# Four layers over one adjacency matrix: the order of the first loads on the sync queue

## The chip, the cores and the metric

One core of a Trainium2 chip runs the whole program. The metric is the device time of one launch in microseconds; beside it stands one execution taken by the hardware profiler. The engines are PE (matrix products), DVE (vector), ACT (scalar), POOL and SP; SP only issues transfers here, ACT issued two in the kernel before, and POOL issues the indirect ones. All transfers run on 16 DMA engines.

## What is computed

A graph of 2708 nodes, 512 features each, with a weighted, sparse adjacency matrix `adj` (2708 x 2708, float32). Four layers, each adds its result to x after a layer norm and a relu:

```
h = relu(layernorm(x));  x = x + L0(h, adj)     # (adj + head) @ h / row sum,  head = mask / |mask|
h = relu(layernorm(x));  x = x + L1(h, adj)     # attention of 8 heads, with Wv and Wo
h = relu(layernorm(x));  x = x + L2(h, adj)     # two adjacency layers and a tanh
h = relu(layernorm(x));  x = x + L3(h, adj)     # (adj != 0) @ (h W + b) / degree
```

The diagonal of `adj` is always there. In L1 the kernel multiplies Wv by Wo once (`wvo`) and reads, for each node, one row of h @ wvo.

## The kernel before, in words

**Tiles.** Nodes are cut into 22 tiles of 128 rows (the last has 20). Layer 0, the part that the change touches, runs a loop over node tiles m from 0 to 21 and needs, for each: the slab `ar` (128 rows of adj, 128 x 2708, 1.39 MB, line 563), from which ACT makes signs (L583), counts and row sums (L611) and DVE the two largest of a row and their places (`attended`, L623 and L624, one pass each); blocks `at` of the transposed adj (128 x 4 x 128, 256 KB, L680), from which DVE makes the left operand `inc` (L698, L706); and the normed rows `h` of x (tiles h0 to h21).

**Three dense tiles, then lists.** For m = 0, 1, 2 (LEAD is 3) the product takes all 22 row tiles: six to seven blocks `at` each, two PE instructions for a row tile (L866). From m = 3 on it takes a few dense row tiles, and the rest is gathered: ranks of nonzero columns (counts by PE at L325, scan at L405, write and read back by SP at L409 and L445, search by DVE at L461) give indices, by which POOL gathers pieces of adj (L635) and rows of h from `h0d` (L654) into the buffers that held h6 to h21. `h0d` is the stored copy of the normed rows (L492, issued by POOL).

**The opening.** Before the loop over m stands a sequence written out by hand. It loads Wv and Wo on the ACT queue (L499, L503), slab 0, four row tiles of x, slab 3, six more tiles of x, slab 4, and the last twelve tiles of x, all on SP (L485, L563). Then it norms rows: statistics on DVE (L194, L196), a square root on ACT (L198), reciprocal and shift on DVE (L199, L201), and the norm with relu on ACT (L204). `value_weights` transposes Wv on PE (L514), copies it to SBUF on DVE (L517), multiplies it by Wo on PE (L176) and copies the product `wvo` out on ACT (L521). `stats_to` does a slab's signs and sums; slabs come in the order 0, 3, 4, 5, 1, 2, 6, 7 and so on.

**What sets the order.** The tile framework takes the operations as the program states them and plans each engine's list ahead, with its own estimate of times; on the chip every engine, and SP's queue too, works its list strictly in order and stands still at the first instruction whose inputs are not there. Slabs have three buffers, blocks `at` three, `inc` three. A transfer also waits until an earlier one that used the same completion counter has landed: transfers of SP and ACT take eight counters in turn, so the ninth waits for the first.

Of the kernel before, what the change touches and what calls it, by code (L numbers as in the profile page):

```python
# [9 lines left out]
FP = mybir.dt.float32  # L10
# [12 lines left out]
P = 128  # L23
# [21 lines left out]
def kernel(  # L45
# [27 lines left out]
    nc = tc.nc  # L73

    N, D = x.shape
    H, _, DK = wk_d.shape
    NT = (N + P - 1) // P
# [12 lines left out]
    def rows(t):  # L90
        return min(P, N - t * P)

    def dense_of(m):

        return WHOLE[m]

    def alone(m):

        return DENSE <= m < NFULL
# [70 lines left out]
    def span(t):  # L170
        return slice(t * P, t * P + rows(t))

    def project(acc, hT, n, w):

        for c in range(NCD):
            nc.tensor.matmul(  # L176
                acc[:n], hT[:, c, :n], w[:, c, :], start=(c == 0), stop=(c == NCD - 1)
            )
# [65 lines left out]
    with tc.tile_pool(name="l0_slab", bufs=2) as slabs, tc.tile_pool(  # L244
        name="l0_h", bufs=1
    ) as hp, tc.tile_pool(name="l0_w", bufs=2) as wp, tc.tile_pool(
        name="l0_acc", bufs=2, space=PSUM
    ) as ps_acc, tc.tile_pool(name="l0_small", bufs=1, space=PSUM) as ps_small, tc.tile_pool(
        name="l0_list", bufs=3, space=PSUM
    ) as ps_list, tc.tile_pool(name="l0_tr", bufs=1, space=PSUM) as ps_tr, tc.tile_pool(  # L250
        name="l0_y", bufs=1, space=PSUM
# [228 lines left out]
        h0 = {}  # L480

        def load_h0(ts):
            for t in ts:
                h0[t] = hp.tile([P, D], FP, name=f"h{t}")
                nc.sync.dma_start(out=h0[t][: rows(t)], in_=x[span(t)])  # L485

        def norm_h0(ts):
# [8 lines left out]
        wo = wset.tile([P, NCD, D], FP, name="wa1")  # L496

        def load_values():
            nc.scalar.dma_start(  # L499
                out=wv.rearrange("p h c k -> p h (c k)"),  # L500
                in_=wv_d.rearrange("h (p c) k -> p h (c k)", c=NCD),
            )
            nc.scalar.dma_start(out=wo, in_=wo_d.rearrange("(c p) k -> p c k", p=P))  # L503

        def value_weights():

            wvo = hp.tile([P, NCD, D], FP, name="wvo")
            wvt = wset.tile([P, NCD, D], FP, name="wa2")
            for r in range(NCD):
                pt = ps_tr.tile([P, NCD, P], FP, name="pt")  # L510
                for c in range(NCD):
                    for k in range(0, P, DK):
                        head = wv[:, (r * P + k) // DK, c, :]
                        nc.tensor.matmul(  # L514
                            pt[k : k + DK, c, :], head, ident, start=True, stop=True
                        )
                nc.vector.tensor_copy(wvt[:, r, :].rearrange("k (p c) -> k c p", c=NCD), pt)  # L517
            for r in range(NCD):
                acc = ps_y.tile([P, D], FP, name="yacc")
                project(acc, wvt[:, :, r * P : (r + 1) * P], P, wo)  # L520
                nc.scalar.copy(wvo[:, r, :], acc)  # L521
            return wvo
# [30 lines left out]
        FIRST = list(range(LEAD, LEAD + GROUP))  # L553
# [4 lines left out]
        def load_slab(m):  # L558
            n = rows(m)
            if m in slab:  # L560
                return
            slab[m] = slabs.tile([P, N], FP, name="ar", bufs=3)
            nc.sync.dma_start(out=slab[m][:n], in_=adj[m * P : m * P + n])  # L563
# [124 lines left out]
        def incidence(m):  # L688

            n = rows(m)  # L690
            rn = row[m][0]
            rb = ps_small.tile([P, P], FP, name="rb")
            nc.tensor.matmul(
                rb[:, :n], rn[:n].to_broadcast([n, P]), ident[:n, :n], start=True, stop=True
            )

            def add_head(inc, a, k, num):
                nc.vector.scalar_tensor_tensor(  # L698
                    inc,
                    a,  # L700
                    0.0,
                    rb[:k, :n].unsqueeze(1).to_broadcast([k, num, n]),
                    op0=ALU.is_gt,
                    op1=ALU.mult,
                )
                nc.vector.tensor_tensor(inc, inc, a, ALU.add)  # L706

            pairs = []
            if m >= LEAD:
                ts = tiles_d[: dense_of(m)]  # L710
                pieces = [ts[i : i + PIECE0] for i in range(0, len(ts), PIECE0)]
            else:
                pieces = in_order if m + 1 < LEAD else dense_last
            for ts in pieces:
                at, k = blocks.pop(m) if m in blocks else load_block(m, ts)
                d = (slice(0, k), slice(0, len(ts)), slice(0, n))
                inc = slabs.tile([P, PIECE0, P], FP, name="inc", bufs=3)
                add_head(inc[d], at[d], k, len(ts))
                pairs += [(inc[:k, i, :n], h0[t][:k]) for i, t in enumerate(ts)]
            if alone(m):  # L720
                c = diag_c[:, m : m + 1]
                by = wp.tile([P, 3], FP, name="by")
                nc.scalar.activation(by[:, 2:3], c, AF.Sign)
                nc.scalar.activation(by[:, 2:3], by[:, 2:3], AF.Identity, scale=rn, bias=c)
                nc.scalar.activation(by[:, :2], kept[:, :, m], AF.Copy, scale=by[:, 2:3])
                own = wp.tile([P, D], FP, name="own", bufs=1)
                nc.scalar.activation(own, xs[m], AF.Relu, scale=by[:, 0:1], bias=by[:, 1:2])
                pairs.append((ident, own))
            if m >= LEAD:
                ac, gs = gathers.pop(m)  # L730
                pending.append(lambda: nc.sync.dma_start(out=listed[m], in_=ac))
                inc = slabs.tile([P, NCL, P], FP, name="incl")[:, : CHUNKS[m], :n]
                add_head(inc, ac, P, CHUNKS[m])

                nc.vector.tensor_tensor(
                    ac[:1, 0, :1], ac[:1, 0, :1], inc[:1, 0, :1], ALU.min
                )
                pairs += [(inc[:, c, :], g) for c, g in enumerate(gs)]
            return pairs
# [22 lines left out]
        def stats_to(m):  # L762


            while normed[0] <= order_n.index(m):
                t = order_n[normed[0]]
                do_next()
                load_slab(t)
                if normed[0] + 1 < NT:
                    load_slab(order_n[normed[0] + 1])  # L770
                row_norm(t)
                row_sum(t)
                if t == 0 or t % GROUP == GROUP - 1 or t >= NT - 2:
                    last_block = count(masks)
                    if t not in ZERO:
                        if dense_of(t):
                            rank_blocks(list(masks), last_block)
                        else:
                            flush_counts()
                            todo.append(partial(rank_rows, list(masks)))  # L780
                        todo.extend(partial(search, k) for k in masks)
                        do_next(0)
                    masks.clear()
                if t in LATE:
                    slab.pop(t)
                else:
                    attended(t)
                normed[0] += 1
# [40 lines left out]
        def flush():  # L829
# [2 lines left out]
                issue()  # L832
            pending.clear()

        load_values()
        load_slab(0)
        load_h0(range(4))
        load_slab(FIRST[0])
        load_h0(range(4, 10))
        load_slab(FIRST[1])  # L840
        load_h0(range(10, NT))
        stats_to(0)
        norm_h0(range(4))
        incs, hns, xs, hTs = {0: incidence(0)}, {}, {}, {}
        stats_to(FIRST[0])
        wvo = value_weights()
        norm_h0(range(4, 10))
        stats_to(FIRST[1])
        norm_h0(range(10, 16))
# [562 lines left out]
    FIRST = 2  # L1412
# [86 lines left out]
    for i, m in enumerate(order_3):  # L1499
# [6 lines left out]
        if i + AHEAD < len(order_3):  # L1506
            k = order_3[i + AHEAD]
# [19 lines left out]
    with tc.If(general > 0):  # L1527

        with tc.tile_pool(name="l0_g", bufs=2) as gp, tc.tile_pool(
            name="l0_gh", bufs=1  # L1530
        ) as hp, tc.tile_pool(name="l0_gps", bufs=2, space=PSUM) as ps:
            hs = []
            for t in range(NT):
# [3 lines left out]
                h = hp.tile([P, D], FP, name=f"h{t}")  # L1537
                norm(gp, xt, n, h, AF.Relu)
                hs.append(h)
            for m in range(NT):  # L1540
# [23 lines left out]
                for t in range(NT):  # L1564
                    k = rows(t)
# [18 lines left out]
        with tc.tile_pool(name="l1_qkv", bufs=1) as qkvp:  # L1584
# [3 lines left out]
            wo = load_w(qkvp, wo_d, "wo")  # L1588
            qk_scale = float(DK) ** -0.5

            with tc.tile_pool(name="l1_pw", bufs=1) as pwp, tc.tile_pool(
                name="l1_ph", bufs=2
            ) as php, tc.tile_pool(name="l1_px", bufs=3) as pxp, tc.tile_pool(
                name="l1_pps", bufs=2, space=PSUM
# [4 lines left out]
                for w, src in ((wk, wk_d), (wq, wq_d), (wv, wv_d)):  # L1599
                    for h in range(H):  # L1600
                        nc.sync.dma_start(
                            out=w[:, :, h * DK : (h + 1) * DK],
                            in_=src[h].rearrange("(c p) k -> p c k", p=P),
# [34 lines left out]
            with tc.tile_pool(name="l1_bias", bufs=2) as bp, tc.tile_pool(  # L1638
                name="l1_p", bufs=2
            ) as pp, tc.tile_pool(name="l1_pT", bufs=3) as ptp, tc.tile_pool(  # L1640
                name="l1_x", bufs=1
            ) as xp, tc.tile_pool(name="l1_st", bufs=4) as stp, tc.tile_pool(
                name="l1_s", bufs=2, space=PSUM
            ) as ps_s, tc.tile_pool(name="l1_t", bufs=2, space=PSUM) as ps_t, tc.tile_pool(
                name="l1_o", bufs=1, space=PSUM
            ) as ps_o, tc.tile_pool(name="l1_y", bufs=1, space=PSUM) as ps_y:
                SW = 2 * BLK
                for m in range(NT):
# [11 lines left out]
                    for h in range(H):  # L1660
                        oc, r0 = divmod(h * DK, P)
                        p = pp.tile([P, N], FP, name="p")
# [21 lines left out]
                        for t0 in range(0, NT, 4):  # L1684
# [3 lines left out]
                            for t in ts:  # L1688
                                k = rows(t)
# [9 lines left out]
                            for t in ts:  # L1699
                                k = rows(t)  # L1700
# [29 lines left out]
        with ExitStack() as gen:  # L1730
# [3 lines left out]
            hp = gen.enter_context(tc.tile_pool(name="hp", bufs=2))  # L1734
# [218 lines left out]
```

## Time and profile before

| | us |
|---|---|
| runs of the kernel before (5) | 1421.26 to 1431.37, median 1429.03 |
| profiled execution, its own time | 1432.48 |
| its span | 1430.7 |
| layer 0, up to the last row combine | 0 to 500 |
| busy in the span: PE, DVE, ACT, POOL | 1216.1, 925.4, 693.7, 675.2 |
| busy from 0 to 80: PE, DVE, ACT, POOL | 53.57, 43.30, 58.27, 17.43 |
| tile 0 combined, tile 1, tile 2, tile 3 (L879) | 79.25, 104.86, 145.89, 170.7 |

A line of the timeline holds start, duration, engine, line, operation, output<-inputs, form and count; in brackets stands the engine's idle time before it and what ended it. A line of the waits holds the waiting instruction, what it waited for, total us, times, and the longest. "SPq" is SP's queue of transfers. From 0 to 80 us the trace counts 28.63 MB moved at a DMA share of 0.98. PE's granted clock is 1.0 in most stretches and 0.5 in short ones.

### The profile page before, as it was taken

What the parts mean: (1) busy time and instruction counts of PE and PEld (TensorE: products, weight loads), DVE (VectorE), ACT (ScalarE), POOL (GpSimd) and SP (SyncE); (2) the same over time, 40 slices, a digit from 0 to 9 for tenths busy, and PEclk for the clock granted to TensorE, in tenths of its full rate; (3) what the DMA queues carried; (4) which work ended last, traced back from release to release, by engine and by line L of the source; (5) the groups of instructions that cost most, each with busy time, mean ns of one, the idle gap of its engine ahead of it and who ended that gap; (6) DMA issues with size and microseconds to landing.
All of it is one profiled execution on the core that took longest, in us unless ns stands there. A gap on an engine that the chain in (4) does not pass through costs nothing. (4 is left out here: it accounts for less than half of the span.)

```text
span 1430.7 us, 15148 instructions
## 1 busy us (share of the span) xinstructions
PE 1216.1 (85%) x4223; PEld 722.0 (50%) x4223; DVE 925.4 (65%) x1859; ACT 693.7 (48%) x1098; POOL 675.2 (47%) x703
## 2 busy tenths in 40 slices
PE   4877976859686938999989999899999999958797
PEld 2333433324333415765655665466656666636575
DVE  4676984859699957963444445456577776737576
ACT  5865353647536446642333223244555554625453
POOL 2255465555558351106554553245435444167663
PEclk9988998889898968999999999999999999979999
DMA  9986887778869659728887878766656656488885
GB/s 340 371 278 229 301 280 236 258 238 309 273 202 319 234 193 318 243 92 267 263 281 233 279 250 258 255 205 201 215 166 217 201 191 208 141 312 253 262 243 168
DMA packets 179341, 349.92 MB, mean 245 GB/s; under 512 B 22794, under 2 KB 85524, under 8 KB 175516
## 3 DMA queue, kind: packets, MB, share of 16 engines
q1 hardware_dynamic: 131648, 201.72, 41.5%
q0 software_dynamic: 46032, 145.05, 31.7%
q10 hardware_dynamic: 1568, 2.10, 0.4%
q8 instruction: 35, 0.57, 0.2%
q14 instruction: 58, 0.48, 0.1%
HBM read 285.97 MB, written 62.82 MB: 244 GB/s over the span
## 5 line engine op out<-in xcount | busy, mean ns | idle before, releaser
L1047 POOL DMA_INDIRECT gg<-g2d,idx_g x130 | 146.2, 1125 | 190.5 <-PE aggs L1110 141.8
L1110 PE MATMUL aggs<-gg,ac 128*128 128x512 f32 (+1 forms) x520 | 231.5, 594 | 2.6 <-DMA gg<-g1d,idx_g 2.5
L1047 POOL DMA_INDIRECT gg<-g1d,idx_g x130 | 131.8, 1014 | 157.1 <-PE aggs L1110 83.4
L635 POOL DMA_INDIRECT ac<-in_adj_t_dram,idx_a x130 | 135.1, 1039 | 94.7 <-issue 45.2
L866 PE MATMUL acc<-h,inc 128*128 128x512 f32 (+1 forms) x276 | 138.8, 647 | 35.1 <-DVE inc L706 28.7
L654 POOL DMA_INDIRECT h<-h0d,idx_g x111 | 113.2, 1020 | 90.0 <-issue 34.4
L1110 PEld LDWEIGHTS aggs<-gg,ac 128*128 128x128 f32 (+1 forms) x520 | 97.4, 189 | 113.1 <-issue 100.0
L866 PE MATMUL acc<-h,incl 128*128 128x512 f32 (+1 forms) x222 | 109.4, 634 | 5.8 <-issue 5.8
L866 PEld LDWEIGHTS acc<-h,inc 128*128 128x128 f32 (+1 forms) x276 | 53.3, 206 | 95.9 <-issue 55.6
L176 PE MATMUL yacc<-wvo,hT 128*128 128x512 f32 (+1 forms) x176 | 87.0, 634 | 7.0 <-ACT hT L211 6.3
L1047 POOL DMA_INDIRECT gg<-hidr,idx_g x62 | 65.6, 1057 | 37.6 <-issue 18.0
L1075 DVE SCALAR_TENSOR_TENSOR ac<-ac,diag_c,bias 128x512 f32<-128x512 f32 x30 | 22.5, 751 | 89.3 <-DMA ac<-g1d 50.4
L1106 PE MATMUL agg<-ghi,a_hi 128*128 128x512 f32 x180 | 76.4, 424 | 0.0
L1106 PE MATMUL agg<-glo,a_lo 128*128 128x512 f32 x180 | 72.6, 403 | 4.4 <-ACT glo L225 4.4
L1106 PE MATMUL aggs<-gs,a_s 128*128 128x512 f32 x180 | 72.5, 403 | 1.7 <-DVE gs L222 1.3
L866 PEld LDWEIGHTS acc<-h,incl 128*128 128x128 f32 (+1 forms) x222 | 43.0, 200 | 57.5 <-issue 53.6
L990 DVE SCALAR_TENSOR_TENSOR v_lo<-pt,v_hi 128x512 fp32r<-128x512 f32 (+1 forms) x88 | 56.9, 657 | 15.3 <-ACT v_hi L989 12.1
L623 DVE MAX8 tops<-ar 128x8 f32<-128x2708 f32 (+1 forms) x22 | 65.3, 2970 | 0.0
L624 DVE FIND_INDEX8 at_top<-tops,ar 128x8 uint32<-128x2708 f32 (+1 forms) x22 | 65.3, 2968 | 0.0
L1139 DVE SCALAR_TENSOR_TENSOR u<-aggs,u 128x512 f32<-128x512 f32 x42 | 28.9, 688 | 53.2 <-PE aggs L1110 39.7
L989 ACT ACTIVATE v_hi<-pt 128x512 fp32r<-128x512 f32 (+1 forms) x88 | 48.2, 575 | 29.2 <-PE pt L983 21.6
L176 PEld LDWEIGHTS yacc<-wvo,hT 128*128 128x128 f32 (+1 forms) x176 | 34.6, 201 | 51.5 <-issue 43.7
(355 smaller groups left out, 2788.3 us busy)
## 6 DMA issues: line engine op xcount, KB each, us to landing
ar<-in_adj_dram SPq DMA_DIRECT2D x27, 1354.0 KB
raw<-in_adj_t_dram SPq DMA_DIRECT2D x92, 192.0 KB
slot<-x SPq DMA_DIRECT2D x41, 256.0 KB
at<-in_adj_t_dram SPq DMA_DIRECT2D x26, 256.0 KB
h<-in_x_dram SPq DMA_DIRECT2D x21, 256.0 KB
h0d<-h POOLq DMA_DIRECT2D x21, 256.0 KB
xt<-in_x_dram SPq DMA_DIRECT2D x21, 256.0 KB
x<-xt SPq DMA_DIRECT2D x21, 256.0 KB
```

The source lines that it names most:

```text
L176: nc.tensor.matmul(acc[:n], hT[:, c, :n], w[:, c, :], start=(c == 0), stop=(c == NCD - 1))
L623: nc.vector.max(tops[:n, m, :], ar[:n])
L624: nc.vector.max_index(at_top[:n, m, :], tops[:n, m, :], ar[:n])
L635: nc.gpsimd.indirect_dma_start(out=ac[:, c, :n], out_offset=None, in_=adj_units, element_offset=dense_of(m) * P * N + m * P, in_offset=bas ...
L654: nc.gpsimd.indirect_dma_start(out=g, out_offset=None, in_=h0d[:, :], in_offset=bass.IndirectOffsetOnAxis(ap=index_g(m)[:, c : c + 1], axi ...
L866: product = nc.tensor.matmul(acc[:n], a, g, start=(i == 0), stop=(i == len(pairs) - 1))
L989: nc.scalar.activation(hi[d], pt[d], AF.Relu, scale=UP)
L990: nc.vector.scalar_tensor_tensor(lo[d], pt[d], 0.0, hi[d].bitcast(FP), op0=ALU.max, op1=ALU.subtract)
L1047: nc.gpsimd.indirect_dma_start(out=gs[c], out_offset=None, in_=gd[:, :], in_offset=bass.IndirectOffsetOnAxis(ap=index_g(m)[:, c : c + 1], ...
L1106: turn(nc.tensor.matmul(acc[:n], a[:k, i, :n], b[:k], start=st, stop=sp))
L1110: nc.tensor.matmul(mixed[:n], a, g, start=(c == 0 and not dense_of(m)), stop=(c == len(chunks) - 1),)
L1139: done = nc.vector.scalar_tensor_tensor(u[:n], mixed[:n], EPS12, u[:n], op0=ALU.mult, op1=ALU.add)
```

## The change

Wv becomes the first transfer of SP's queue instead of ACT's. Wo goes to SP as well, behind the first four tiles of x. The request for slab 4 and for the last twelve tiles of x is stated behind slab 0's statistics, the norm of the first four tiles and the operand of tile 0, so that the first blocks `at` of tile 0 are requested ahead of those twelve. `value_weights` is stated ahead of slab 3's statistics instead of behind. The buffers h0 to h21 are made in front of all loads, since the operand of tile 0 names them.

```diff
         def load_h0(ts):
             for t in ts:
-                h0[t] = hp.tile([P, D], FP, name=f"h{t}")
                 nc.sync.dma_start(out=h0[t][: rows(t)], in_=x[span(t)])
...
         def load_values():
-            nc.scalar.dma_start(
+            nc.sync.dma_start(
                 out=wv.rearrange("p h c k -> p h (c k)"),
                 in_=wv_d.rearrange("h (p c) k -> p h (c k)", c=NCD),
             )
-            nc.scalar.dma_start(out=wo, in_=wo_d.rearrange("(c p) k -> p c k", p=P))
+
+        def load_output():
+            nc.sync.dma_start(out=wo, in_=wo_d.rearrange("(c p) k -> p c k", p=P))
...
+        for t in range(NT):
+            h0[t] = hp.tile([P, D], FP, name=f"h{t}")
         load_values()
         load_slab(0)
         load_h0(range(4))
+        load_output()
         load_slab(FIRST[0])
         load_h0(range(4, 10))
-        load_slab(FIRST[1])
-        load_h0(range(10, NT))
         stats_to(0)
         norm_h0(range(4))
         incs, hns, xs, hTs = {0: incidence(0)}, {}, {}, {}
+        load_slab(FIRST[1])
+        load_h0(range(10, NT))
+        wvo = value_weights()
         stats_to(FIRST[0])
-        wvo = value_weights()
         norm_h0(range(4, 10))
```

FIRST is the list 3, 4, 5. The order that the framework plans from this, on SP: Wv, slab 0, x 0 to 3, Wo, slab 3, x 4 to 9, three blocks of tile 0, slab 4, three more blocks (the third of one row tile), x 10 to 16, the seventh block, x 17 to 21, slab 5, slab 1. Before, it was: slab 0, x 0 to 3, slab 3, x 4 to 9, slab 4, x 10 to 21, three blocks, slab 5, three more blocks, slab 1, the seventh block. On the other engines the planned order differs as well, in all of layer 0 up to about tile 18.

## The prediction, as it was put on record

> **What bounds the kernel now.** I started from the page's busy rows and then cut the span into its stages. Layer 0 fills 0 to 500 us, and only there does the built order of instructions differ between the two kernels (on DVE the last difference stands near row 656 of some 4630, at node tile 18 of 0 to 21; behind it both run the same list). So the question is what limits layer 0, above all its opening. Busy time of stretches of the kernel before; the columns are busy us (and instructions) of PE, weight load, DVE, ACT and POOL, then granted clock, DMA share and GB/s:
>
> ```profile
> 12.00:24.00 12.00, 7.00 (x48) 4.50 (x48) 3.75 (x12) 2.91 (x6) 0.00 (x0) 1.00 0.91 330
> 24.00:80.00 56.00, 46.57 (x140) 18.22 (x139) 36.07 (x125) 49.17 (x78) 11.92 (x22) 0.91 1.02 373
> 99.00:125.00 26.00, 14.37 (x32) 5.62 (x34) 14.27 (x30) 7.61 (x14) 17.20 (x19) 0.74 0.58 182
> 125.00:146.00 21.00, 18.55 (x57) 8.28 (x54) 13.52 (x20) 14.37 (x17) 8.97 (x10) 0.84 0.88 302
> ```
>
> The reader is to see three things. From 24 to 80 us ACT works 49.17 of 56 us and the DMA share is 1.02: both are close to full. From 12 to 24 us ACT works 2.91 of 12 us, so 9.1 us are open there. From 99 to 125 us nothing is full: PE 14.37 of 26, ACT 7.61, DMA 0.58.
>
> Why ACT stands still before 24 us is told by the waits of the opening (PE, then SP's queue) and by the timelines of DVE and ACT:
>
> ```profile
> PE pt L514 <- DMA wa<-in_L_gnn_Wvs_dram: 15.9, 1, 15.9
> ...
> SPq L485 <- DMA wa<-in_L_gnn_Wvs_dram: 11.8, 1, 11.8
> ```
> ```profile
> 17.87 1.05 DVE L517 COPY wa<-pt 128x512 f32<-128x512 f32 x1 [5.69 <-PE pt L514]
> 18.77 0.15 DVE L585 TENSOR_SCALAR sum_sgn<-sum_sgn 128x1 f32<-128x1 f32 x1
> ```
> ```profile
> 13.48 0.19 ACT L611 ACTIVATION_READ_ACCUMULATOR ar<-ar 128x1 f32 x1
> 19.04 0.29 ACT L588 ACTIVATE rn<-sum_sgn,tiny 128x1 f32<-128x1 f32 x1 [5.37 <-DVE kept L199]
> 23.05 0.57 ACT L341 CAST counts<-list 128x485 bf16<-128x485 f32 x1 [3.72 <-PE list L325]
> ```
>
> Read backwards: ACT waits 5.37 us for a small DVE result; DVE cannot reach it because the copy of the transposed Wv (L517) stands in front and waits 5.69 us for PE; PE waits for Wv until 15.86. ACT's second wait, 3.72 us, is for the counts of slab 0, which stand on PE behind the same Wv products. SP is held too: its fifth row of x waits 11.8 us until Wv has landed.
>
> **The change part by part.** Time is counted against the profiled execution: span 1430.7 us, time 1432.48 us. It lies 3.45 us over the median of the runs, 1429.03; the sum is made on the former and taken off the latter.
>
> *Wv to the head of SP's queue.* In the DMA view of 0 to 80 us, the ACT queue (q10), which carries Wv and Wo alone, takes 7.5% of 16 engines: 0.075 x 80 = 6.0 us for both, 3.0 us for Wv. Placed first, Wv pushes slab 0 back by at most that: the first sign (L583) starts at 7.06 + 3.0 = 10.06 us instead of 7.06. This is a cost. The DVE statistics that stand behind the Wv copy now follow within that time, and the waits of 5.37 and 3.72 us go. From 10.06, ACT works through what it did from 7.06 to 13.67 (6.61 us, to 16.7), then rn 0.29, counts 0.83, three norms of x with their square roots 3 x 0.75 + 0.8 = 3.1, and is at slab 3's sign at 20.9 us. Slab 3 has to be there: in front of it lie Wv, slab 0, four rows of x and Wo, with itself 1.05 + 1.39 + 1.05 + 1.05 + 1.39 = 5.93 MB, at 0.36 MB/us (q1: 20.93 MB in 72.9% of 80 us) 16.5 us on top of a start near 2 us: 18.5 us. It is. Before, that sign started at 24.97 with one norm done. So ACT is 24.97 - 20.9 = 4.1 us earlier and two norms (1.5 us) further: **5.6 us** ahead. If slab 0 were not delayed at all it would be 8.6; if slab 3 came 3 us later than worked out, 2.6.
>
> *What is late next.* From there ACT has the same work up to slab 6's sign (79.74 us before): 49.17 us of 56. The 6.8 us of waits inside (the largest: counts 2.59 for PE and 1.73 for a store of counts, kept 1.56) may stay or shrink. The DMA queue is next: it moved 28.7 MB in 80 us at a share of 0.98, so for ACT to be 5.6 us earlier it must move nearly all of that in 74 us, up to 0.388 MB/us, where 60 to 80 us ran at 0.383. It can only just follow, so I take 1.1 us off: **4.5 us**, ends 0 and 8.6.
>
> *Wo behind four rows of x.* It lands near 15 us (4.54 MB at 0.36 plus 2), where SP's wait for it ended at 18.41 before; the product that needs it has its first copy of wvo at 32.34 us. Hidden; if not, it is the 3.0 us of Wo once.
>
> *First adj blocks ahead of the last twelve rows of x.* Three blocks of 256 KB, slab 4, then three more blocks (one short) pass in front of rows 10 to 21 on SP. The blocks of m = 0 were issued from 32.82 to 52.79 us. DVE can start them at about 27 us instead of 42.57, while it waits for rows anyway; PE then multiplies rows as their norm comes from ACT, so tile 0 ends when ACT has normed the last rows, as now. No gain of its own beyond ACT's. The price: SP's blocks 4 to 7 wait for the buffers of 1 to 3 (three buffers), and twelve rows of x queue behind them. Covered by slab 4's 3.9 us of transfer, 0; uncovered, the 3.5 us which SP lost on such a block before.
>
> *Slab 5, ranks, first gather.* With fewer norms between (the order has 6 instead of 11 behind slab 5's sign, 5 x 1.1 us), the ranks of tiles 3 to 5 and the first gather on POOL (85.30 us before) come some 10 us earlier. Worth nothing alone: the gathers of rows wait for PE to release the rows of x (2.11 us at 131.32, 15.4 us once later).
>
> *Node tile 2, 99 to 146 us.* Before, slab 8 (issued 88.33) stood ahead of tile 2's first block (90.05), and DVE sat idle 2.87 us up to 102.45 before it could build it; PE lost 5.84 and 6.07 us on DVE there. After, that block goes ahead of slab 8, but slab 9, which waits for slab 6's maxima, goes ahead of the next two blocks, and DVE does slab 7's two passes (2.98 + 2.97 us) before them. The first saves up to 5.84 us; the second costs up to slab 9's 3.9 us of transfer. Bounds: 12 us gained (both PE waits go), 10 us lost (one further wait of slab plus two passes). The rows seen nearest are 2.9 to 6.1 us; I take **4 us gained**, because POOL's gathers, which share the DMA engines with these blocks, will be further on.
>
> Sum: 4.5 + 4 = **8.5 us**. From 146 to 200 us PE is busy 51.19 of 54, so what is gained by then starts that stretch earlier and is carried on: 1429.03 - 8.5 = 1420.5.
>
> The Trainium skill speaks against a gain from the queue alone ("DMA: Bandwidth & Descriptors", section Issuing engines are not separate DMA queues): transfers from all issuers share the same 16 engines and interleave, so only issue time is saved. By it Wv's move would be worth about 0. This trace shows interleaving is not neutral in order: Wv and slab 0 were issued together at 0.75 us, slab 0 was used at 7.06 and Wv at 15.86. By the row the move is worth the 4.5 us above; I follow the row.
>
> **Rivals.**
> - *The opening is limited by its bytes.* The same 28.7 MB pass either way at a share of 0.98, and ACT's 9.1 us turn into later waits for slabs 4, 5 and rows. For it: share 1.02 from 24 to 80 us. Against: SP stood 11.8 us, and from 16 to 24 us the queues moved only 0.30 MB/us. Gain 0 to 4: 1425 to 1429.
> - *A new wait in tile 2* (other side). SP's in-order queue sets blocks 2 and 3 of tile 2 behind slab 9, which waits for slab 6 to be done on DVE; DVE's order then sets slab 8's passes ahead of blocks 4 and 5. Price: 3.9 us of slab and 5.95 us of passes, and once more for the next pair: up to 19.7 us, less the opening's 4.5, so 2 to 15 us lost. It decides from the point where PE's waits on DVE's inc in tile 2 exceed the present 11.9 us by over 4.5. 1431 to 1444. The same mechanism could strike a later tile, since the order of all of them up to 18 is new.
> - *More than the sum.* Both waits of tile 2 go (11.9 us) and a stretch like 200 to 260 us, where PE is busy 37.7 of 60, packs better by a few: 1408 to 1416.
> - *The opening is not early at all*: slab 0's 3 us are lost and ACT then waits for slab 3. Then 0 to +3 us; it is counted with the first rival.
>
> **How the numbers follow.** Forecast (4.5 to 13 us gained, 1416 to 1424.5) 0.40; bytes 0.20; new wait 0.28; more 0.12. A measurement of this kernel can tell about 0.5%, 7.1 us, from no change: 1421.9 and 1436.2. Under 1421.9 lie seven tenths of the forecast, 0.28, and all of "more", 0.12: faster 0.40. Over 1436.2 lie five sixths of the new wait, 0.23. The rest, 0.37, is within. The range leaves out half of "more" (0.06) and the upper half of the new wait (0.14): 1409 to 1438. Cases of both signs hold much of the chance; the forecast's own range is 1416 to 1424.5.
>
> **What would show it.** Right: PE's first product starts at 6 us, not 15.86; slab 0's sign near 10, slab 3's near 21, slab 6's near 75 us; POOL's first gather near 75; ACT busy about 10 of the 12 us from 12 to 24; tile 2's combine (145.89 before) near 137. Wrong: slab 4's or 5's sign waits for its DMA by over 2 us (bytes); PE idle in tile 2 over 16 us on inc (new wait); or the lead at 146 us is gone by 500 us though tile 2 had it, which would mean that another chain than ACT's and PE's sets layer 0.

## The result and the profile after

The changed kernel takes **1430.44 us** (median of 44 runs, 1416.88 to 1444.12); the kernel before takes 1429.65 us (86 runs). The ratio is **1.0009, 95% interval [0.9992, 1.0026]**: no measurable change, where 8.5 us were forecast. Run once more on another chip it gave 0.9987 [0.9956, 1.0019]. The profiled execution takes 1433.39 us with a span of 1431.6 (before 1432.48 and 1430.7). Ratios leave out runs that are over 1.5% above the fastest of their kernel; medians in us are of all runs. Against the kernel before, lines of the changed kernel are numbered one lower from L485 to L499, one higher from L503 on, and four higher from L850 on.

The four stretches of before, now in the changed kernel (PE, weight load, DVE, ACT, POOL, clock, DMA share, GB/s):

```profile
12.00:24.00 12.00, 9.38 (x48) 5.09 (x48) 6.77 (x22) 9.24 (x16) 1.67 (x3) 1.00 1.05 388
24.00:80.00 56.00, 40.08 (x103) 16.35 (x103) 34.02 (x120) 45.82 (x71) 11.74 (x20) 0.85 0.91 328
99.00:125.00 26.00, 18.62 (x62) 7.42 (x60) 17.55 (x31) 12.14 (x19) 10.72 (x12) 0.80 0.78 265
125.00:146.00 21.00, 10.83 (x37) 4.71 (x31) 11.40 (x21) 20.85 (x22) 10.81 (x11) 0.82 0.77 248
```

The hole in front of 24 us is filled: ACT is busy 9.24 of 12 us (2.91 before). But from 24 to 80 us ACT falls from 49.17 to 45.82 and the DMA share from 1.02 to 0.91, and PE, 18.55 us busy from 125 to 146 before, now has 10.83.

The waits of the opening (PE, then SP's queue), the copy of the transposed Wv on DVE, and four of ACT's instructions:

```profile
PE pt L515 <- DMA wa<-in_L_gnn_Wvs_dram: 6.3, 1, 6.3
```
```profile
SPq L484 <- DMA wa<-in_L_gnn_Wvs_dram: 0.5, 1, 0.5
```
```profile
8.33 1.05 DVE L518 COPY wa<-pt 128x512 f32<-128x512 f32 x1 [5.91 <-PE pt L515]
```
```profile
9.69 2.46 ACT L584 ACTIVATE sgn<-ar 128x2708 bf16<-128x2708 f32 x1 [7.66 <-DMA ar<-in_adj_dram]
...
22.72 2.44 ACT L584 ACTIVATE sgn<-ar 128x2708 bf16<-128x2708 f32 x1
...
52.73 2.44 ACT L584 ACTIVATE sgn<-ar 128x2708 bf16<-128x2708 f32 x1
...
81.85 2.46 ACT L584 ACTIVATE sgn<-ar 128x2708 bf16<-128x2708 f32 x1 [2.00 <-DMA ar<-in_adj_dram]
```

Wv is there at 6.3 instead of 15.9 us, SP's wait of 11.8 us for it is 0.5, slab 0's sign is at 9.69 as the sum said, slab 3's at 22.72 (24.97 before). But slab 5's sign, 48.40 before, stands at 52.73, with sixteen norms done ahead of it instead of eleven, and slab 6's, with the same work done in both, at 81.85 (79.74 before), after a wait of 2.00 us for the slab itself: the lead is lost on the way.

Then node tile 2. What PE waits for there (99 to 158 us), before and in the changed kernel:

```profile
PE acc L866 <- DVE inc L706: 11.9, 2, 6.1
```
```profile
PE rb L694 <- DVE inc L699: 10.2, 1, 10.2
PE acc L870 <- DVE inc L707: 5.9, 2, 5.5
```

SP's queue, its longest wait, the stretches from 130 us on (columns as above), DVE and PE in the changed kernel:

```profile
129.56 0.33 SPq L564 DMA_DIRECT2D ar<-in_adj_dram  x1
130.66 1.22 SPq L681 DMA_DIRECT2D at<-in_adj_t_dram  x2
132.14 2.26 SPq L409 DMA_DIRECT2D rank_b<-rk  x4
144.53 0.35 SPq L445 DMA_DIRECT2D ranks<-rank_b  x1
146.64 0.94 SPq L681 DMA_DIRECT2D at<-in_adj_t_dram  x2
```
```profile
SPq L445 <- DMA rank_b<-rk: 10.0, 1, 10.0
```
```profile
130.00:134.00 4.00, 4.00 (x11) 1.58 (x9) 2.80 (x10) 4.00 (x5) 3.13 (x3) 1.00 1.01 323
134.00:138.00 4.00, 1.83 (x7) 0.67 (x6) 2.06 (x3) 4.00 (x5) 2.95 (x4) 1.00 0.98 341
138.00:142.00 4.00, 0.00 (x0) 0.00 (x0) 1.27 (x1) 4.00 (x6) 1.89 (x2) 0.58 1.06 374
```
```profile
126.56 2.97 DVE L625 FIND_INDEX8 at_top<-tops,ar 128x8 uint32<-128x2708 f32 x1
129.45 0.72 DVE L699 SCALAR_TENSOR_TENSOR inc<-at,rb 128x384 f32<-128x384 f32 x2
...
144.66 0.69 DVE L699 SCALAR_TENSOR_TENSOR inc<-at,rb 128x512 f32<-128x512 f32 x1 [5.38 <-DMA at<-in_adj_t_dram]
145.59 0.42 DVE L699 SCALAR_TENSOR_TENSOR inc<-at,rb 128x256 f32<-128x256 f32 x1 [0.25 <-DMA at<-in_adj_t_dram]
145.93 1.02 DVE L707 TENSOR_TENSOR inc<-inc,at 128x512 f32<-128x512 f32 x2
```
```profile
146.07 0.79 PE L694 MATMUL rb<-ident,rn 128*128 128x128 f32 x2 [10.23 <-DVE inc L699]
```

Read backwards: PE stands 10.23 us until DVE has passed over tile 2's last two blocks, the sixth (144.66) and the seventh (145.59), and DVE waits 5.38 us for the sixth. Both were requested from 130.66 on. They need buffers that DVE frees with the operands of blocks 4 and 5 (129.45), and these stand behind the second pass over slab 8 (126.56 to 129.53). Slab 11, whose request waits for the same pass, goes ahead of them at 129.56. The sixth block then takes 14 us to come, at a DMA share of 0.98 to 1.06. PE's other long wait there, 5.50 us up to 119.11, is for operands that DVE makes behind both passes over slab 7 (111.21 to 117.27).

SP's own longest wait is another one: it stores the ranks, the next entry of its list reads them back, and it stands 10.0 us until the store has landed. In tile 2 this holds up nothing: the two blocks behind the read are of tiles 3 and 4, and they go out at 146.64 and 147.13, as soon as DVE has freed their buffers (L707, 145.93 to 146.95).

Tile 2 is combined at 156.92 instead of 145.89. Of these 11.0 us, 4.4 were there at tile 1 (109.22 against 104.86), and 6.7 come in tile 2. Yet tile 3 is only 1.0 us late, and the last combine of layer 0 is 3.8 us early.

### The profile page after: what moved, and what is told of

The parts are those of the page before. It is cut to its first block, busy times and chain, and to the rows that moved or that the text cites. A ratio compares the mean times of both kernels' runs of the same rounds, so it can differ in the third digit from the quotient of the medians.

```text
span 1431.6 us, 15146 instructions
## 1 busy us (share of the span) xinstructions
PE 1219.5 (85%) x4223; PEld 724.7 (51%) x4223; DVE 925.0 (65%) x1859; ACT 692.8 (48%) x1098; POOL 667.4 (47%) x703
## 5 line engine op out<-in xcount | busy, mean ns | idle before, releaser
L1051 POOL DMA_INDIRECT gg<-g2d,idx_g x130 | 141.0, 1085 | 198.3 <-PE aggs L1114 145.0
L870 PE MATMUL acc<-h,inc 128*128 128x512 f32 x276 | 142.3, 656 | 28.4 <-DVE inc L707 24.6
L636 POOL DMA_INDIRECT ac<-in_adj_t_dram,idx_a x130 | 129.4, 996 | 78.2 <-issue 44.7
L870 PE MATMUL acc<-h,incl 128*128 128x512 f32 (+1 forms) x222 | 106.0, 627 | 0.0
L870 PEld LDWEIGHTS acc<-h,inc 128*128 128x128 f32 x276 | 53.0, 207 | 86.5 <-issue 48.5
L994 DVE SCALAR_TENSOR_TENSOR v_lo<-pt,v_hi 128x512 fp32r<-128x512 f32 (+1 forms) x88 | 56.9, 656 | 15.9 <-ACT v_hi L993 15.7
L1014 PE MATMUL main<-wb,v_hi 128*128 128x512 f32 (+1 forms) x176 | 56.9, 446 | 4.1 <-ACT v_hi L993 2.5
```

The source lines that it names most:

```text
L636: nc.gpsimd.indirect_dma_start(out=ac[:, c, :n], out_offset=None, in_=adj_units, element_offset=dense_of(m) * P * N + m * P, in_offset=bas ...
L870: product = nc.tensor.matmul(acc[:n], a, g, start=(i == 0), stop=(i == len(pairs) - 1))
L994: nc.vector.scalar_tensor_tensor(lo[d], pt[d], 0.0, hi[d].bitcast(FP), op0=ALU.max, op1=ALU.subtract)
L1014: nc.tensor.matmul(acc[:n], a[:, c, :n], b[:, c, :], start=first and c == 0, stop=last and c == NCD - 1,)
L1051: nc.gpsimd.indirect_dma_start(out=gs[c], out_offset=None, in_=gd[:, :], in_offset=bass.IndirectOffsetOnAxis(ap=index_g(m)[:, c : c + 1], ...
```

## The experiments

Sixteen runs on four chips, each kernel against runs of before on its own chip. On three chips, called the slower ones here, before takes 1432.16, 1427.84 and 1435.09 us, on a fast one 1355.19. The planner writes new lists for the middle of layer 0 for nearly every edit. Some kernels turned out to have the same lists on every engine behind the opening (about 80 us; on ACT one to three short instructions stand elsewhere up to about 118 us) and otherwise differ in the opening alone. They are what separates the two theories. **Theory O**: the lead or delay of the opening is carried to the end. **Theory P**: the time follows the planned lists of the middle. (The first four expectations were written before the lists were compared: A says that the middle has slack, B that two halves of the change cancel, and C is O.)

### First chip: the parts alone

`e1_weights`, of the diff only this:

```diff
         def load_values():
-            nc.scalar.dma_start(
+            nc.sync.dma_start(
...
-            nc.scalar.dma_start(out=wo, in_=wo_d.rearrange("(c p) k -> p c k", p=P))
+        def load_output():
+            nc.sync.dma_start(out=wo, in_=wo_d.rearrange("(c p) k -> p c k", p=P))
...
         load_h0(range(4))
+        load_output()
```

> The kernel before, with only the weights moved: Wv first on the sync queue and Wo behind four rows of x. The blocks of adj stay where they were. Theory A (slack: what the opening gains or loses up to node tile 2 is used up by waits in the middle of layer 0, and the end does not move): ScalarE reaches the sign of slab 3 2 to 4 us earlier than the 24.97 us of before and the time stays within 4 us of before. Theory B (two halves that cancel: the weights gain what the blocks lose): the time is 4 us or more below before, and the sign of slab 5 stays at 48.4 us or comes earlier. Theory C (the opening is carried to the end in full, but the move only permutes work that ScalarE and the transfers have to do anyway): slab 6's sign within 2 us of 79.74 us, and the time within 3 us.

Measured: 0.9947 [0.9912, 0.9982]. Faster by 7.6 us, as B said; but slab 5's sign is 1.6 us late, where B had it no later, and slab 6's 0.6 us late, so the gain is not a lead of the opening.

`e2_blocks`, the other half: the weights stay on ACT's queue, `value_weights` stays behind slab 3 (h0 to h21 are made ahead, as in the change).

```diff
...
-        load_slab(FIRST[1])
-        load_h0(range(10, NT))
         stats_to(0)
         norm_h0(range(4))
         incs, hns, xs, hTs = {0: incidence(0)}, {}, {}, {}
+        load_slab(FIRST[1])
+        load_h0(range(10, NT))
```

> The kernel before, with only the first blocks of adj, slab 4 and the last twelve rows of x in the new order; both weights stay on ScalarE's queue and their products stay behind slab 3's statistics. Theory A: tiles 0 to 2 move by some us (the sign of slab 5 from 48.4 us to 51 to 53 us), the time stays within 4 us of before. Theory B: the time is 4 us or more above before. Theory C: the time moves by what slab 6's sign moves, to within 3 us.

Measured: 0.9996 [0.9962, 1.0029]; slab 5's sign 5.2, tile 0 7.9, tile 2 10.4 us late, much as in the changed kernel, and the time is that of before: B falls, the halves do not cancel. Its lists behind the opening are those of the changed kernel. With these lists the move of the weights and of the value product makes 1.0009 out of 0.9996: nothing measurable.

`e7_no_weights`:

```diff
         def load_values():
-            nc.scalar.dma_start(
...
-            nc.scalar.dma_start(out=wo, in_=wo_d.rearrange("(c p) k -> p c k", p=P))
+            nc.vector.memset(wv, 0.01)
+            nc.vector.memset(wo, 0.01)
```

> The kernel before without the transfers of Wv and Wo: both tiles are filled with a constant by VectorE instead, and so layer 0's value product is computed from the constant (it leaves these two inputs out). It shows the most that any place for the two transfers can gain. The transfers took 7.5 per cent of 16 queues in 80 us, 6.0 us. Theory A: ScalarE's sign of slab 3 comes 5 us earlier than at 24.97 us, and the time stays within 4 us of before. Theory B: 6 us or more below before. Theory C: 4 to 7 us below before, by as much as slab 6's sign is earlier.

Measured: 0.9909 [0.9873, 0.9944]; 13.0 us, within B's 6 or more and above C's 4 to 7; slab 3's sign is 7.2 and slab 6's 8.1 us early, the end of layer 0 14.1.

`e8_late`:

```diff
         load_slab(0)
         load_h0(range(4))
+        for _ in range(4):
+            nc.vector.tensor_copy(slab[0], slab[0])
```

> The kernel before, with slab 0 of adj copied onto itself four times by VectorE between its landing and its first use: a delay of 4 times 1.5 to 3 us (a pass of VectorE over a slab, MAX8, takes 2.97 us), 6 to 12 us, for the first sign on ScalarE. Theory A: the signs of slabs 0 and 3 are late by most of it, node tile 0 by less, and the time is within 4 us of before. Theory B says nothing of its own here. Theory C: the time is longer by nearly the whole delay that is left at slab 6's sign, 5 to 10 us.

Measured: 0.9932 [0.9886, 0.9978]. The first sign is 8.1 us late, and the kernel is faster, by 9.7 us. C had it slower and falls; A had it within 4 us, which the interval (3.2 to 16.3 us) just touches. That its lists are new, as those of the kernels above, led to theory P.

### Second chip: kernels with equal lists

`e6_weights_values`: `e1_weights` with the value product stated earlier, so the change without the move of the blocks.

```diff
+        wvo = value_weights()
         stats_to(FIRST[0])
-        wvo = value_weights()
```

> The kernel before with the weights moved to the sync queue and the value product stated ahead of slab 3's statistics, but with the blocks of adj where they were. Behind the opening, its planned lists on all engines are the same as those of the kernel without the two transfers, which took 0.9909 of before. So the two form a pair: the same lists behind the opening, once with 2.1 MB of weights and once without. Theory P (the time follows which lists the planner wrote for the middle of layer 0; what the opening gains or loses is mostly not carried): ratio to before 0.987 to 0.995, as without the weights. Theory O (the opening's lead or delay is carried): the weights cost their 6.0 us of queue time again, and the ratio is 0.994 to 0.999.

Measured: 0.9928 [0.9891, 0.9965], next to 0.9909 [0.9873, 0.9944] without any weights: as P said, though the interval reaches into O's 0.994 to 0.999. And the opening does here what the prediction had said of the whole change (ACT's signs of slabs 3, 5 and 6, and the stretches up to 80 us):

```profile
22.00 2.44 ACT L584 ACTIVATE sgn<-ar 128x2708 bf16<-128x2708 f32 x1
...
48.78 2.44 ACT L584 ACTIVATE sgn<-ar 128x2708 bf16<-128x2708 f32 x1
...
74.81 2.46 ACT L584 ACTIVATE sgn<-ar 128x2708 bf16<-128x2708 f32 x1
```
```profile
12.00:24.00 12.00, 8.63 (x48) 4.63 (x48) 7.50 (x25) 10.04 (x16) 1.68 (x3) 1.00 1.04 410
24.00:80.00 56.00, 47.32 (x118) 18.75 (x118) 36.29 (x121) 49.52 (x76) 10.30 (x19) 0.91 1.00 357
```

Slab 6's sign is at 74.81 (forecast near 75), ACT is full in both stretches. Against 81.85 in the changed kernel, the move of the blocks costs 7.0 us there (one execution each; another one of the changed kernel had 84.08).

`e3_slab5_ahead`, on the changed kernel:

```diff
-        load_h0(range(10, NT))
+        load_h0(range(10, 16))
+        load_slab(FIRST[2])
+        load_h0(range(16, NT))
```

> The changed kernel with one more slab of adj (slab 5) asked for ahead of the last six rows of x. It undoes what the new order of the blocks did to slab 5, whose sign came at 52.73 us instead of 48.40. Its lists in the middle of layer 0 are again new: behind the store of the second ranks stands one block of adj, and only then the read of the ranks, where the changed kernel has the read first and two blocks behind it. Theory P: the time is set by that order: the wait of 10.2 us that TensorE has in tile 2 of the changed kernel is gone and the ratio to before is 0.990 to 0.997. Theory O: slab 5's sign comes back by 4 us and the time goes with it, ratio 0.997 to 0.999; if slab 5 does not come earlier, 1.001.

Measured: 0.9984 [0.9951, 1.0018]. Slab 6's sign is at 74.93 and tile 0 5.5 us ahead of before: the place of slab 5's request, at 43.31 in the changed kernel, at 35.44 here and at 35.11 in `e6_weights_values`, was the loss of the opening. The time did not move measurably: the wait of 10.2 us in tile 2 is gone, and another list brings others (PE 9.4 us for ACT's counts). The ratio lies in O's 0.997 to 0.999 and above P's 0.990 to 0.997, but the interval reaches into P's range and over 1: this run does not decide between them.

`e15_more_bytes`, on the changed kernel:

```diff
         load_values()
+        for i in range(3):
+            more = slabs.tile([P, NCL, P], FP, name="ac", bufs=3)
+            nc.scalar.dma_start(
+                out=more.rearrange("p c k -> p (c k)"), in_=adj[i * P : i * P + P, : NCL * P]
+            )
         load_slab(0)
```

> The changed kernel with three more transfers on ScalarE's queue at the start: 128 x 1024 numbers of adj each, 1.57 MB in all, into buffers that are written again before anyone reads them. Behind the opening, every engine's list is that of the changed kernel. 1.57 MB at the 0.36 MB/us of the opening are 4.4 us. Theory P: signs and tile 0 come 2 to 5 us later than in the changed kernel, tile 3's combine within 3 us, the time within 3 us of it, so a ratio to before of 0.998 to 1.003. Theory O: the time is 4 to 5 us over the changed kernel's, ratio 1.003 to 1.007.

Measured: 1.0032 [0.9999, 1.0066], the changed kernel 1.0009: just inside O's range, with most of P's in the interval, so undecided. In the two profiles tile 0 is 4.4 us later than in the changed kernel, tile 2 2.5, the last combine 0.7.

`e4_values`, on the kernel before:

```diff
+        wvo = value_weights()
         stats_to(FIRST[0])
-        wvo = value_weights()
```

> The kernel before with only the value product stated ahead of slab 3's statistics. No transfer is moved, and it is the third part of the change alone. The lists behind the opening are new, those of no other kernel. Theory P: anything from 0.988 to 1.003, with the signs of slabs 0 and 3 within 2 us of before, and the sign of the ratio told by the waits between tiles 1 and 4 and not by the opening. Theory O: nothing moves in the opening, ratio 0.998 to 1.002.

Measured: **0.9890 [0.9848, 0.9933]**, 15.7 us, and no transfer was moved. O had 0.998 to 1.002 and falls. Nor is it a lead of the opening; slab 6's sign on ACT, 79.74 before:

```profile
87.51 2.44 ACT L583 ACTIVATE sgn<-ar 128x2708 bf16<-128x2708 f32 x1
```

The opening is 7.8 us **late** at slab 6, tile 0 is 1.1 us late, and the last combine of layer 0 is 22.0 us early. The profiled executions side by side (us; before, then the difference to it):

| | slab 3's sign | slab 6's sign | tile 0 | tile 2 | last combine | ratio |
|---|---|---|---|---|---|---|
| before | 24.97 | 79.74 | 79.25 | 145.89 | 499 | 1 |
| changed | -2.2 | +2.1 | +6.2 | +11.0 | -3.8 | 1.0009 |
| weights | -1.3 | +0.6 | -0.7 | -5.1 | -15.4 | 0.9947 |
| blocks | +0.7 | +4.2 | +7.9 | +10.4 | +0.2 | 0.9996 |
| weights, values | -3.0 | -4.9 | -3.7 | -5.5 | -21.3 | 0.9928 |
| values | +0.6 | +7.8 | +1.1 | -5.7 | -22.0 | 0.9890 |
| no weights | -7.2 | -8.1 | -2.2 | -10.3 | -14.1 | 0.9909 |
| slab 0 late | -1.0 | -1.9 | +5.5 | +8.4 | -5.2 | 0.9932 |
| slab 5 ahead | -1.6 | -4.8 | -5.5 | +1.8 | -9.8 | 0.9984 |

Neither slab 6's sign nor tile 0 tells the sign of the ratio. An early tile 2 goes with a faster kernel; a late one goes with no measurable change, and once (slab 0 late) with a faster kernel too. One execution is worth no more than some 8 us here: `e4_values`, run again below, had its last combine 14.1 us early.

### The fast chip, and a third slower one

Four more kernels ran on a chip on which before takes 1355.19 us. `e16_one_more_first` is before with one useless transfer (the edit below), `e17_before_more` and `e18_values_more` are before and `e4_values` with three on POOL's queue (the edit of `e15_more_bytes`, `nc.gpsimd` for `nc.scalar`), `e5_values_late` is the changed kernel with `value_weights` back behind slab 3.

```diff
+        for i in range(1):
+            more = slabs.tile([P, NCL, P], FP, name="ac", bufs=3)
+            nc.sync.dma_start(
+                out=more.rearrange("p c k -> p (c k)"), in_=adj[i * P : i * P + P, : NCL * P]
+            )
         load_values()
         load_slab(0)
```

`e16_one_more_first`:

> The kernel before with one useless transfer as the first of the sync queue: 128 x 1024 numbers of adj, 0.52 MB, into a buffer that is written again before it is read. It is pure extra work, 1.5 us at the 0.36 MB/us of the opening. Behind the opening, its planned lists are those of the kernel without weights and of the one with weights and values moved, which took 0.9909 and 0.9928 of before. Theory P (the time follows the lists of the middle of layer 0): ratio 0.988 to 0.996, so faster by extra work. Theory O (the opening's lead or delay is carried): ratio 1.000 to 1.002.

`e17_before_more`:

> The kernel before with three useless transfers of 0.52 MB each, 1.57 MB in all, on GpSimd's queue at the start. All other lists stay exactly those of before. 1.57 MB at 0.36 MB/us are 4.4 us. Theory P: signs up to slab 6 and tile 0 later by 2 to 5 us, ratio 0.998 to 1.003. Theory O: ratio 1.003 to 1.004, and the whole of the delay at tile 0 is still there at the end of layer 0.

`e18_values_more`:

> The kernel with only the value product stated earlier (0.9890 of before) and the same three useless transfers on GpSimd's queue. All other lists stay those of that kernel. Its opening is then later than that of before by some 4 us more than the 1 to 8 us it already was. Theory P: ratio 0.987 to 0.994. Theory O: 0.992 to 0.994 at the best, since 4.4 us come on top.

`e5_values_late`:

> The changed kernel with the value product back behind slab 3's statistics: weights and blocks of adj moved, values not. Behind the opening, all its lists are those of the changed kernel, of the kernel with the blocks alone, and of the one with more bytes. Theory P: ratio 0.998 to 1.003, like these three. Theory O: as slab 6's sign stands, within 3 us.

Measured: 0.9981 [0.9954, 1.0009]; 1.0045 [1.0017, 1.0073]; 1.0069 [1.0044, 1.0093]; 1.0081 [1.0055, 1.0107]. P's ranges miss all four (the intervals of the first two touch them). O's miss too, the second by little (1.0045 against 1.003 to 1.004): where the lists equal those of before, 1.57 MB cost 6.1 us (2.3 to 9.9), with 4.4 us estimated from their bytes. Here the delay seems to be carried. The lists of `e4_values`, with the same bytes, have no gain left (1.0069 against 1.0045), and those of the changed kernel lose 11 us.

Bytes or chip? The next four put kernels of both groups on one chip; it was one of the slower kind.

`e19_after_again`:

> The changed kernel once more. If the chip is one on which the kernel before takes 1428 to 1432 us: ratio 0.997 to 1.004, as before. If it takes near 1355 us: theory P with a chip's own times (which lists are good depends on how fast the chip works them) says 1.004 to 1.010, since the kernel with the same lists behind the opening stood at 1.0081 there; theory P without the chip says 0.998 to 1.003.

`e20_values_again`:

> The kernel with only the value product stated earlier, once more. On a chip with 1428 to 1432 us for before: 0.985 to 0.994 again. On one near 1355 us: if the chip turned the gain around, 0.999 to 1.005 (the 1.0069 of the same lists with 1.57 MB more, less the 4.5 us that these bytes cost the kernel before); if the bytes did, 0.985 to 0.994.

`e21_before_more_again`:

> The kernel before with 1.57 MB of useless transfers, once more. On a chip with 1428 to 1432 us for before, theory P: 0.998 to 1.003; theory O (the opening's delay is carried in full): 1.003 to 1.005. On one near 1355 us: 1.0017 to 1.0073 again.

`e22_values_more_again`:

> The kernel with the value product stated earlier and 1.57 MB of useless transfers, once more. On a chip with 1428 to 1432 us for before, theory P: 0.986 to 0.996, the gain of the lists kept with the opening later than that of before by 5 to 11 us; theory O: over 1.000. On one near 1355 us: 1.004 to 1.010 again.

Measured: the changed kernel 0.9987 [0.9956, 1.0019]; values earlier **0.9905 [0.9870, 0.9939]**; before with 1.57 MB more 0.9962 [0.9919, 1.0006]; values earlier with 1.57 MB more 0.9909 [0.9866, 0.9952]. The first, second and fourth are as on the other slower chips, so it was the chip and not the bytes. The third missed the ranges of P and of O, on the fast side, and is not firm: its twelve runs go from 1416.15 to 1454.29 us, and the median of all, 1436.30, is above the 1435.09 of before. On two chips of the slower kind the lists of `e4_values` are worth about 1%, with more bytes still 0.6 (by the median of all, 1426.29) to 0.9%; on the fast one they are worth nothing.

| lists behind the opening | openings, on the slower chips | on the fast chip |
|---|---|---|
| before's | +1.57 MB 0.9962 | +1.57 MB 1.0045 |
| the changed kernel's | changed 1.0009, 0.9987; blocks alone 0.9996; +1.57 MB 1.0032 | values late 1.0081 |
| a third | no weights 0.9909; weights and values 0.9928 | 0.52 MB more 0.9981 |
| `e4_values`' | 0.9890, 0.9905; +1.57 MB 0.9909 | +1.57 MB 1.0069 |

Along a row the openings differ by 1 to 6 us at slab 6's sign and the ratios by up to 0.5%, which is too coarse to say whether those few us are carried. Down the first column the ratios differ by 1% with the lists, against their openings: that rules O out as the cause of these differences, on the slower chips. The version faster than both kernels on the slower chips is `e4_values`; alone, it was not run on the fast one.

## Why the prediction was wrong, by its own steps

- **Wv to the head of the queue**: right. Slab 0's sign 9.69 (forecast 10.06), Wv's wait 15.9 to 6.3, SP's 11.8 to 0.5.
- **ACT 5.6 us ahead at slab 3's sign**: half. It came at 22.72, not 20.9, with three norms done as worked out: 2.25 + 1.5 = 3.8 us. ACT still waits 2.73 us for a norm's numbers from DVE.
- **"The waits inside may stay or shrink", 4.5 us at slab 6**: failed, by the term that was put at nothing, **"first adj blocks ahead of the last twelve rows"**. Its price was given as 0, uncovered 3.5 us; it was 7.0 us (81.85 against 74.81 with the blocks left in place). What was late next was not a row of x but slab 5, whose request stands behind all of them (43.31, before 36.09); `e3_slab5_ahead` moves that request alone and has 74.93. The 4.5 us themselves were sized well: 4.9 and 4.8 in these two kernels. In the first of them the DMA share is 1.04 and 1.00 in the two stretches of the opening, with the lead there, so the rival that the bytes use it up falls too.
- **Node tile 2, 4 us gained**: failed, 6.7 lost (from tile 1's combine to tile 2's 47.70 us instead of 41.03), and 11.0 with what came from tile 1. The rival "a new wait in tile 2" had the mechanism and the place. Slab 9 goes ahead of blocks 2 and 3 (100.77; 101.19 and 104.40), slab 8's passes go ahead of the operands of blocks 4 and 5, and slab 11 ahead of blocks 6 and 7. PE waits 16.1 us on operands there, 11.9 before; the rival's sign was 16. The reason for the gain, that POOL's gathers would be further on, did not hold: POOL issued eleven of them from 126.51 to 139.42, beside the last blocks. All runs of the changed kernel's lists have PE's wait at the last two blocks (8.9 to 10.7 us, on the fast chip 10.2). What the rival had wrong is that the loss stays.
- **"What is gained by then starts that stretch earlier and is carried on"**: failed, and it weighs most on these chips. The argument was one stretch with PE 51.19 of 54 busy. 11.0 us lost at tile 2 are 1.0 at tile 3 and a gain at the end; with other lists 5 to 10 us gained at tile 2 grow to 14 to 22 by the last combine, and in `e4_values` 7.8 us lost at slab 6 end 22.0 ahead. From 200 to 400 us PE is busy 148.36 of 200 us before (76.59 and 71.77): there is room there in which the lists decide. I had read that their order was new up to tile 18 and priced it only as a rival. That the time came out where it was before is the net of terms that failed, foreseen by none of them.
- **Rule and row**: with equal lists, Wv and Wo first, with the value product stated earlier, are worth 2 to 3 us up to slab 6 (-2.2 against +0.7 at slab 3, +2.1 against +4.2 at slab 6) and no measurable time. On the time the rule of the Trainium skill ("DMA: Bandwidth & Descriptors", section Issuing engines are not separate DMA queues) stood nearer than the row that I followed; in the opening itself the order does count.

**What stays open.** Which entries of `e4_values`' lists bring the 1% is not shown. One candidate: PE's wait at the rank product L403 from 90 to 500 us is 28.8 us in before and 2.2 in `e4_values`; but in the kernel with the weights alone, which is faster too, it is 24.3, and in `e15_more_bytes`, which is not faster, 7.0. Why the 11.0 us of tile 2 are 1.0 at tile 3 was not followed. Whether a pure delay is carried on the slower chips is open as well (-5.5, +3.3 and +0.6 us for 1.57 MB, each uncertain by 5 to 8; +1.2 and +6.3 for the first and the last by medians of all runs). In the profiles with the lists of before it was: `e21_before_more_again` is 5.7 us behind before at tiles 0, 2 and 3 and 5.6 at the last combine (an execution of 1439.16 us, one of its longer ones). With the changed kernel's lists 4.4 us at tile 0 became 0.7, and two executions of `e4_values` itself lie 7.9 us apart there.

## What to carry to other kernels

Where a planner writes the lists, an edit in the opening is two changes: the opening, and every list behind it. Compare lists before pricing rows, and look for a kernel with the edit's opening and the old lists, or the reverse, before a gain or a loss is put down to the edit. A lead is worth something only if the stretch behind it is full up to the point where the time is measured; and the longest wait of a queue need not be the one that costs. Follow a wait back from the engine that stands to the very transfer that ended it: SP's 10.0 us held nothing that was needed, while the block that PE stood for had been asked for before them.

## What the runs showed of the hardware that was not expected

**One kernel, two kinds of chip.** On three chips before takes 1428 to 1435 us, on a fourth 1355. `e17_before_more` there has the lists of before and an opening 7.2 us later at tile 0, and its last combine of layer 0 is 57.1 us earlier. Layer 0 from 200 to 300 us, before on a slower chip, then that kernel on the fast one:

```profile
200.00:300.00 100.00, 76.59 (x205) 34.65 (x206) 69.72 (x128) 48.53 (x71) 57.02 (x59) 0.85 0.78 260
```
```profile
200.00:300.00 100.00, 95.18 (x302) 43.70 (x300) 93.37 (x181) 72.40 (x100) 75.36 (x77) 0.98 0.99 349
```

Of the same list 302 recorded PE instructions fall into these 100 us instead of 205, at a granted clock of 0.98 instead of 0.85; up to the last combine both traces record 1124. One stretch of PE's list, the counts of a group of slabs and what follows, on the slower chip, with ACT's copy that waits for them, and on the fast one:

```profile
238.14 2.27 PE L325 MATMUL list<-sgn,counts 128*32 128x512 bf16 x28
241.57 0.24 PE L325 MATMUL list<-sgn,counts 128*32 128x192 bf16 x1 [1.16 <-issue]
242.97 0.24 PE L325 MATMUL list<-sgn,counts 128*32 128x192 bf16 x1 [1.16 <-issue]
245.07 1.01 PE L866 MATMUL acc<-h,incl 128*128 128x512 f32 x1 [1.86 <-issue]
247.87 1.01 PE L866 MATMUL acc<-h,incl 128*128 128x512 f32 x1 [1.78 <-issue]
250.67 1.01 PE L866 MATMUL acc<-h,incl 128*128 128x512 f32 x1 [1.79 <-issue]
252.07 1.01 PE L866 MATMUL acc<-h,incl 128*128 128x512 f32 x1 [0.39 <-issue]
256.58 0.58 PE L403 MATMUL list<-sums,ahead_of 128*128 128x1 f32 x2 [3.51 <-DVE rk L399]
```
```profile
255.02 0.59 ACT L341 CAST counts<-list 128x512 bf16<-128x512 f32 x1 [17.38 <-remote]
```
```profile
219.47 2.27 PE L325 MATMUL list<-sgn,counts 128*32 128x512 bf16 x30
221.67 1.98 PE L871 MATMUL acc<-h,incl 128*128 128x512 f32 x4
223.67 0.38 PE L403 MATMUL list<-sums,ahead_of 128*128 128x1 f32 x2
```

From the counts to the rank product it is 4.2 us on the fast chip and 18.4 on the other. There, from 240 to 252 us, recorded PE instructions start 1.4 to 2.8 us apart, whether they take 0.24 or 1.01 us, with a granted clock of 0.50 from 245 to 260 us. ACT waits 17.38 us, up to 255.02, to copy the counts, though the last of them on PE is recorded at 242.97; "remote" means that the profile names no engine for the end of this wait. "Issue" means that the profile shows nothing that PE waited for. None of the four profiles of the fast chip has a PE idle time ended by "issue" in layer 0; the profiles of the slower chips have 10 to 39 us of it each. What causes it was not tried. That these stretches sit at other places in other lists would fit that the lists' worth is of the slower chips alone; it is not shown.
